# Last feed-forward group multiplied with the tokens on the partitions: an attention and feed-forward block in one kernel

## The chip, the cores and the metric

The kernel runs on one core of a Trainium2 chip. The metric is the device time of one execution in microseconds (us). The core has a matrix engine, TensorE (PE in the profile; its weight loads are listed as PEld), a vector engine, VectorE (DVE), a scalar engine, ScalarE (ACT), GpSimd (POOL), and SyncE (SP), whose queue issues all DMA transfers here. Each engine works through its own instructions in order and waits on semaphores for the others. SBUF is the on-chip memory with 128 partitions, PSUM the accumulator memory that TensorE writes, in eight banks of 512 float32 per partition.

## The reference

The input is 16 sequences of 256 tokens with 256 features, all float32. One block is computed:

```
x = x + layernorm(attention(layernorm(x)))    # 16 heads of 128, causal, biases on q, k, v and the output
x = x + layernorm(ffn(layernorm(x)))          # 256 -> 2048 -> 256, weights stored as 4-bit codes with scales

q, k, v = x @ W_Q[h] + b_Q[h], ...            # per head
attn    = softmax(causal(q k^T / sqrt(128)))
out     = sum over heads of (attn v) @ W_O[h] + b_O

gate, up = x @ Wg^T, x @ Wu^T
out      = (gelu(gate) * up) @ Wd^T
```

Layernorm has no gain and no bias.

## The kernel before

**Splitting.** [...] Each operand is held as a high part (rounded by a copy) and a low part (the operand minus its high part), and `mm3` (L352) issues three matmuls: high by high, high by low, low by high. Products that stay whole float32, such as one 128x128 block of the scores, are issued as one matmul that the profile lists as two instructions.

**Order.** The kernel writes every engine's order out by hand. `run` (L95) issues each instruction behind the last one of every engine, so that the order in the program is the order on each engine; `dma` (L86) does the same for the transfers, all on SyncE's queue. Side work sits in queues of jobs (`urgent`, `behind`, `spare` and others), from which `slot` takes a step at fixed places.

**Attention.** The 4096 tokens are eight blocks of 512 (two sequences). A unit is one head of one block; there are N = 128, numbered by u. The loop at L1021 runs a pipeline over the units: `st_s` makes the scores and the softmax of unit i + 4 (GpSimd scales the probabilities, tile pr), `st_t` and `st_w` turn them in 32x32 pieces and through DRAM, `st_b` loads them as pt, `st_p` (L481) splits pt of unit i + 1 into ph and pl, `st_z` (L490) multiplies unit i with v into pz and splits the result into zh and zl, and `st_o` adds a head's output product. In `st_p`, ScalarE copies 128x512 numbers to ph and GpSimd subtracts to pl. In the last units the feed-forward part begins between them: `x_ops` splits its input, and the first products run (tiles pa, pd, pf).

**Feed-forward.** Four super-blocks of 1024 tokens (two blocks, bb = 0 and 1) by eight groups of 256 hidden features give 32 groups k (loop L1079). The products of gate and up for the four quarters (two halves c of the hidden features by two blocks) are formed by seven products m1 to m7 instead of eight. `Two.done` sends each quarter through a chain: VectorE adds, ScalarE applies gelu, VectorE multiplies by up, ScalarE copies the high part (CAST inter), VectorE subtracts to the low part. The steps wait in the queue `pending`; `part` issues one or two of them with each product, and `quarter` (L868) issues what a later product needs. `st_d(k, bb, dh)` (L877) multiplies group k's quarters by the down weights, six matmuls of 512 tokens, and adds them to a PSUM bank that holds output features (half dh) on the partitions and tokens along the free axis: banks po0 and po1 for block 0, pv and pz for block 1.

**The end.** In the last super-block group 31 isn't multiplied by `st_d` but in `st_last` (L918). It first issues what is left in `pending`: at that point the cast and the low part of quarter (c = 0, bb = 1), then the gelu, the product, the cast and the low part of quarter (c = 1, bb = 0). Then it takes four half blocks n (block 1's two, then block 0's two) of 256 tokens. `multiply` adds the last group's products for one dh into the bank, six matmuls of 256 tokens, and ScalarE copies the 128x256 result to SBUF (oT). `turn_and_measure` turns four 128x128 pieces back with TensorE (transposes into tpo), and VectorE takes the layernorm statistics (bn_stats, bn_aggr, adding epsilon), GpSimd the power -0.5. `apply` computes nb on VectorE, scales and adds the residual x1 on VectorE (xs), adds the shift on ScalarE and issues the output: one transfer of 256 KB for each of the first three halves, two of 128 KB for the last. Statistics of half n - 1 lie between the two products of half n, and half n - 2 is applied behind them.

Of the kernel before, what the change touches and what calls it, by code (L numbers as in the profile page):

```python
# [10 lines left out]
F32 = mybir.dt.float32  # L11
# [3 lines left out]
AF = mybir.ActivationFunctionType  # L15
# [3 lines left out]
P = 128  # L19
# [9 lines left out]
def kernel(  # L29
# [30 lines left out]
    def f(ap):  # L60
        return ap.bitcast(F32)
# [24 lines left out]
    def dma(dst, src):  # L86
        if queue[0] is None:
            queue[0] = nc.sync.dma_start(dst, src).ins
            return
        with tc.issue_after(queue[0]):  # L90
            queue[0] = nc.sync.dma_start(dst, src).ins
# [3 lines left out]
    def run(op, dst, *args, **kw):  # L95
        with ExitStack() as behind:
            for m in last.values():
                behind.enter_context(tc.issue_after(m))
            ins = op(dst, *args, **kw)  # L99
        last[ins.ins.engine] = ins.ins  # L100
        return ins
# [23 lines left out]
    def add(jobs, job, kind):  # L125
        jobs.append([job, 0, kind])
# [24 lines left out]
    def half(t, b, hf):  # L151
        r = b * TB + hf * S
        return t[r : r + S, :].rearrange("(t p) d -> p t d", p=P)

    def ln_stats(srcs):

        n = len(srcs)
        st = small.tile([P, 4, 6], F32, tag="st", name="st")
        mv = small.tile([P, 4, 2], F32, tag="mv", name="mv")
        rs = small.tile([P, 4], F32, tag="rs", name="rs")  # L160
        for t in range(n):
            run(nc.vector.bn_stats, st[:, t, :], srcs[t])
            if t % 2:
                yield V_
        for t in range(n):
            run(nc.vector.bn_aggr, mv[:, t, :], st[:, t, :])
        run(nc.vector.tensor_scalar, rs[:, :n], mv[:, :n, 1], EPS, None, ALU.add)
        yield G_
        run(nc.gpsimd.tensor_tensor, rs[:, :n], rs[:, :n], mhalf[:, :n], ALU.pow)
        return mv, rs  # L170
# [23 lines left out]
    def wide(name):  # L194
        return work.tile([P, 4, D], F32, tag="wide", name=name, bufs=4)
# [156 lines left out]
    def mm3(o, terms, passes=STATIONARY_LAST, start=True, stop=True, shared=False, lows_last=False):  # L352

        todo = [(lhs(a), rhs(c)) for lhs, rhs in terms for a, c in passes]
        if lows_last:
            todo = [todo[m] for m in (0, 1, 3, 4, 2, 5)]
        for i, (lhs, rhs) in enumerate(todo):
            run(
                nc.tensor.matmul, o, lhs, rhs, start=start and i == 0, stop=stop and i == len(todo) - 1, skip_group_check=shared
            )  # L360
# [120 lines left out]
    def st_p(u):  # L481
        pt = PT.pop(u).rearrange("p a m i -> p m a i")
        ph = work.tile([P, 2, 2, P], F32R, tag="ph", name="ph")
        pl = work.tile([P, 2, 2, P], F32R, tag="pl", name="pl")
        four = [t.rearrange("p c b (a i) -> p (c b) a i", a=4) for t in (ph, pl)]
        run(nc.scalar.copy, four[0], pt[:, 0:4])
        run(nc.gpsimd.tensor_tensor, four[1], pt[:, 0:4], f(four[0]), ALU.subtract)
        PH[u] = (ph, pl, pt)

    def st_z(u):  # L490
# [386 lines left out]
    def st_d(k, bb, dh):  # L877


        if not 0 <= k < NGRP:  # L880
            return
        sb, g = divmod(k, NG)
        b = 2 * sb + bb
        w = FW[k, "d"]
        tags = (("po0", "po1"), ("pv", "pz"))[bb]
        if g == 0:
            ACC[b, dh] = ps.tile([P, TB], F32, tag=tags[dh], name="pd")
        po = ACC[b, dh]
        cols = slice(dh * P, (dh + 1) * P)
        i = [quarter(k, c, bb) for c in range(2)]  # L890
        mm3(
            po, [(lambda a, c=c: w[:, a, c, cols], lambda s, c=c: i[c][:, s]) for c in range(2)], MOVING_LAST,
            start=g == 0, stop=g == NG - 1, shared=True,
        )
        if g == NG - 1:
            if dh == 0:
                ACC[b] = back_tile()
            back(ACC[b], dh, po)
            if dh == 1:
                add((urgent, behind)[bb], end(b, ACC.pop(b)), N_)  # L900

    def end(b, tr):
# [12 lines left out]
        for hf in range(2):  # L915
            dma(half(out, b, hf), X1[b][hf])

    def st_last():  # L918


        k = NGRP - 1
        while pending:
            run(*pending.popleft())
        w = FW[k, "d"]
        halves = [(bb, hf) for bb in (1, 0) for hf in range(2)]
        oTs, os, stats = {}, {}, {}

        def multiply(n, dh):
            bb, hf = halves[n]
            tok = slice(hf * S, (hf + 1) * S)  # L930
            cols = slice(dh * P, (dh + 1) * P)
            i = [quarter(k, c, bb) for c in range(2)]
            po = ACC[2 * NSB - 2 + bb, dh][:, tok]
            mm3(
                po, [(lambda a, c=c: w[:, a, c, cols], lambda s, c=c: i[c][:, s, tok]) for c in range(2)], MOVING_LAST,
                start=False, shared=True,
            )
            if dh == 0:
                oTs[n] = wide("oT").rearrange("p a b -> p (a b)")[:, 0 : 2 * S].rearrange("p (h n) -> p h n", h=2)
            run(nc.scalar.copy, oTs[n][:, dh], po)  # L940

        def turn_and_measure(n):
            tp = ps.tile([P, 2, D], F32, tag=("pk", "pq", "sc", "sc")[n], name="tpo", bufs=2 if n > 1 else 1)
            oT = oTs.pop(n)
            for t in range(2):
                for dh in range(2):
                    run(
                        nc.tensor.transpose,
                        tp[:, t, dh * P : (dh + 1) * P], oT[:, dh, t * P : (t + 1) * P], ident,
                    )  # L950
            os[n] = [tp[:, t, :] for t in range(2)]
            jobs = deque()
            stats[n] = None

            def measure():
                stats[n] = yield from ln_stats(os[n])

            add(jobs, measure(), V_)
            finish(jobs)

        def apply(n):
            bb, hf = halves[n]
            b = 2 * NSB - 2 + bb
            mv, rs = stats.pop(n)
            nb = ln_shift(mv, rs, 2)
            x1 = X1[b][hf]
            for t in range(2):
                run(
                    nc.vector.scalar_tensor_tensor,
                    x1[:, t, :], os[n][t], rs[:, t : t + 1], x1[:, t, :], ALU.mult, ALU.add,  # L970
                )
                run(nc.scalar.activation, x1[:, t, :], x1[:, t, :], AF.Identity, bias=nb[:, t : t + 1])
                if n == len(halves) - 1:
                    dma(half(out, b, hf)[:, t, :], x1[:, t, :])
            if n < len(halves) - 1:
                dma(half(out, b, hf), x1)

        count = len(halves)
        for n in range(count + 2):
            if n < count:  # L980
                multiply(n, 0)
            if 0 <= n - 1 < count:
                turn_and_measure(n - 1)
            if n < count:
                multiply(n, 1)
            if n >= 2:
                apply(n - 2)


    first = first_tokens()  # L990
# [84 lines left out]
    def parts(k, *names):  # L1075
        for name in names:
            part(k, name)

    for k in range(NGRP):  # L1079
        sb, g = divmod(k, NG)  # L1080
        if g == 2 and sb + 1 < NSB:
            while not {(0, 2 * sb + 2), (0, 2 * sb + 3)} <= ready:
                step(behind)
            add(spare, x_ops(sb + 1), N_)
        if g == NG - 1:
            for b in (2 * sb, 2 * sb + 1):
                X1[b] = [x_load(x1d, b, hf, ("pr", "tr")[b % 2]) for hf in range(2)]
        if k > 0:
            parts(k, "m1", "m2")
        st_d(k - 1, 1, 0)  # L1090
        for at, n in (k, "d"), (k + 1, "g"), (k + 1, "u"):
            f_get(at, n)
        slot(V_)
        slot(A_ + G_)
        if k > 0:
            parts(k, "m6")
            parts(k, "m5")
        slot(V_)
        slot(A_ + G_)
        st_d(k - 1, 1, 1)  # L1100
        slot(V_)
        slot(A_ + G_)
        if k > 0:
            parts(k, "m7", "m3")
        if k == NGRP - 1:
            parts(k, "m4")
        st_d(k - 1, 0, 0)
        slot(V_)
        slot(A_ + G_)
        if k < NGRP - 1:  # L1110
            parts(k, "m4")
        st_d(k - 1, 0, 1)
        slot(V_)
        slot(A_ + G_)
    finish(urgent)
    finish(behind)
    st_last()


# [49 lines left out]
```

## Time and profile before

| | us |
|---|---|
| median of 3 runs (1517.84 to 1518.86) | 1517.89 |
| the profiled execution | 1517.91 |
| its span, first to last instruction | 1516.1 |
| TensorE busy | 1498.9 |
| VectorE, ScalarE, GpSimd busy | 1185.8, 1037.0, 728.9 |
| last matmuls (transposes of half 3) begin | 1508.61 |
| last output transfer issued | 1513.2 |

The mean granted clock of TensorE is 0.998. Rows of the profile give a start, a duration, the engine, the line, the operation, "out<-in" by tile names, the shape and a count, and in brackets the engine's idle time before it with what ended it. Because all instructions go through the helper `run`, their line is L99 throughout, and a step is known by its tiles: pl is the low part of the probabilities, inter a quarter's high or low part, pd the output banks, oT the copied sums, tpo the turned ones, st, mv, rs and nb the statistics, xs or x1 the residual. Matmuls overlap in the rows; the distance of their starts is what one costs.

### The profile page before, as it was taken

The page shows a single profiled execution, that of the slowest core. Times are in us where ns is not written, and L with a number is a line of the kernel's source. Part 1 is how long each engine was busy: PE and PEld are TensorE (multiplying, and loading weights), DVE is VectorE, ACT ScalarE, POOL GpSimd, SP SyncE. Part 2 cuts the span into 40 slices and gives each one's busy share as a digit, 9 for nine tenths or more (in the row PEclk, how much of TensorE's full clock was granted, in tenths as well). Part 3 has the DMA queues.
Part 4 walks back from the last instruction along what each step waited for, and adds up shares of the span by engine and source line. Part 5 has one row for each costly group of instructions (what it writes and reads, how often), then busy time and mean ns, then how long its engine had stood idle before and what let it go on. Part 6 is the DMA issues. An engine that isn't in the chain of part 4 may idle for free.

```text
span 1516.1 us, 25754 instructions
## 1 busy us (share of the span) xinstructions
PE 1498.9 (99%) x7831; PEld 1278.7 (84%) x7831; DVE 1185.8 (78%) x3011; ACT 1037.0 (68%) x2614; POOL 728.9 (48%) x951
## 2 busy tenths in 40 slices
PE   8999999999999999999999999999999999999997
PEld 7888888888888888888888888887888888888886
DVE  6876787787787888788778787777887887787866
ACT  6877766777677677676677767676766665666565
POOL 3755578677667776866876876880000000000000
PEclk9999999999999999999999999999999999999999
DMA  8998899999899999899899999977557465655561
GB/s 292 339 319 264 262 305 312 286 306 312 281 294 326 282 315 310 274 318 305 274 285 314 306 296 320 316 239 272 210 193 262 182 248 196 250 180 198 219 233 58
DMA packets 200426, 407.55 MB, mean 269 GB/s; under 512 B 21472, under 2 KB 128480, under 8 KB 189536
## 3 DMA queue, kind: packets, MB, share of 16 engines
q1 hardware_dynamic: 200288, 405.91, 79.9%
q8 instruction: 62, 1.02, 0.3%
q14 instruction: 76, 0.62, 0.1%
HBM read 294.15 MB, written 111.67 MB: 268 GB/s over the span
## 4 chain that ended last, share of the span: by engine, by line
PE 94%; DVE 2%; ACT 1%; DMA 1%; POOL 1%; issue 1%; SPq 0%; POOLq 0%; DVEq 0%; ACTq 0%
PE pd L99 13%; PE pk L99 11%; PE pv L99 11%; PE pq L99 11%; PE po L99 11%; PE pz L99 10%; PE sc L99 9%; PE pa L99 8%; PE pf L99 5%; PE pe L99 2%; DVE sum L99 1%; DMA rawq<-in_wq 0%; DMA rawv<-in_wv 0%; ACT pr L99 0%; DVE inter L99 0%
## 5 line engine op out<-in xcount | busy, mean ns | idle before, releaser
L99 POOL TENSOR_SCALAR pr<-pr,rc 128x128 f32<-128x128 f32 (+1 forms) x512 | 250.1, 504 | 90.7 <-DVE rc L99 90.7
L99 ACT ACTIVATE pr<-sc,mn 128x128 f32<-128x128 f32 (+1 forms) x512 | 208.2, 419 | 87.5 <-DVE mn L99 87.5
L99 POOL TENSOR_TENSOR rs<-rs,mhalf 128x4 f32<-128x4 f32 (+1 forms) x35 | 34.5, 985 | 485.1 <-DVE rs L99 275.0
L99 POOL TENSOR_TENSOR pl<-pt,ph 128x512 fp32r<-128x512 f32 x128 | 165.0, 1289 | 190.0 <-ACT ph L99 178.0
L99 DVE CUSTOM_DVE_ANT_0 sc<-sc,mask 128x128 f32<-128x128 f32 (+1 forms) x512 | 180.8, 374 | 67.8 <-PE sc L99 59.1
L99 PE MATMUL pv<-wv,xT 128*128 128x512 f32 x768 | 208.9, 407 | 0.0
L99 ACT ACTIVATE zh<-pz,bqk 128x512 fp32r<-128x512 f32 x128 | 88.3, 690 | 167.7 <-PE pz L99 167.6
L99 PE MATMUL pk<-xT,wk 128*128 128x512 f32 x768 | 199.5, 395 | 0.3 <-POOL xT L99 0.2
L99 PE MATMUL pd<-inter,wd 128*128 128x512 f32 (+1 forms) x792 | 197.8, 385 | 1.4 <-ACT inter L99 1.0
L99 PE MATMUL pq<-xT,wq 128*128 128x512 f32 x768 | 196.3, 391 | 0.0
L99 PEld LDWEIGHTS pd<-inter,wd 128*128 128x128 f32 x792 | 144.9, 188 | 34.5 <-DVE inter L99 2.9
L99 PEld LDWEIGHTS pq<-xT,wq 128*128 128x128 f32 x768 | 144.2, 188 | 32.9
L99 ACT COPY part<-pa 128x512 f32<-128x512 f32 x192 | 111.6, 585 | 68.0 <-PE pa L99 65.5
L99 PE MATMUL po<-zh,wo 128*128 128x512 f32 x512 | 157.7, 389 | 0.0
L99 PEld LDWEIGHTS pk<-xT,wk 128*128 128x128 f32 x768 | 134.9, 188 | 23.8 <-POOL xT L99 0.7
L99 PEld LDWEIGHTS pv<-wv,xT 128*128 128x128 f32 x768 | 135.0, 189 | 23.6
L99 DVE SCALAR_TENSOR_TENSOR zl<-pz,bqk,zh 128x512 fp32r<-128x512 f32 x128 | 95.9, 749 | 74.0 <-ACT zh L99 73.9
L99 ACT CAST inter<-sum 128x512 fp32r<-128x512 f32 x128 | 80.1, 626 | 87.5 <-DVE sum L99 87.5
L99 DVE TENSOR_TENSOR inter<-sum,inter 128x512 fp32r<-128x512 f32 x128 | 89.0, 695 | 56.9 <-ACT inter L99 55.9
L99 DVE STREAM_TRANSPOSE tr<-pr 128x768 f32<-128x768 f32 x128 | 123.3, 963 | 1.7 <-DMA hop<-tr 1.2
L99 DVE SCALAR_TENSOR_TENSOR kl<-pk,bqk,kh 128x512 fp32r<-128x512 f32 x128 | 96.1, 751 | 30.7 <-ACT kr L99 26.9
L99 PEld LDWEIGHTS po<-zh,wo 128*128 128x128 f32 x512 | 96.0, 188 | 19.9
(149 smaller groups left out, 3723.0 us busy)
## 6 DMA issues: line engine op xcount, KB each, us to landing
hop<-tr SPq DMA_DIRECT2D x512, 96.0 KB
pt<-hop SPq DMA_DIRECT2D x128, 384.0 KB
wk<-wk SPq DMA_DIRECT2D x64, 512.0 KB
wq<-wq SPq DMA_DIRECT2D x64, 512.0 KB
wo<-wo SPq DMA_DIRECT2D x64, 512.0 KB
wu<-fu SPq DMA_DIRECT2D x32, 1024.0 KB
wg<-fg SPq DMA_DIRECT2D x32, 1024.0 KB
wv<-wv SPq DMA_DIRECT2D x56, 512.0 KB
```

Of the source, the lines that this page charges most:

```text
L99: ins = op(dst, *args, **kw)
```

## The change

There are two edits.

1. In `st_p`, the low part pl of the last four units (u >= 124) is computed by VectorE instead of GpSimd.
2. The last group's products are formed with the tokens on the partitions. The sums of groups 0 to 30 are copied whole to SBUF by ScalarE (`copy_last(bb)`, two copies of 128x512) and turned by `base_last(bb)`: eight float32 matmuls against the identity for each block, which write four 128x128 pieces into each of two banks (`BASE`), 128 tokens by 256 features twice. `multiply` then adds group 31's products to these banks with the hidden values as the stationary operand and the down weights (256 wide) as the moving one: twelve matmuls for each half block. The statistics read the banks. The copies of each half's result and its transposes are gone. `copy_last(1)` stands behind block 1's last `st_d`, `base_last(1)` behind m4, `copy_last(0)` ahead of `st_last`, and `base_last(0)` behind the products of half 1.

`apply` changes too. For halves 0 to 2 ScalarE computes the scaled and shifted value from PSUM into a new tile fa, and the residual is added by GpSimd (the first piece of every half and the second of half 2) or by VectorE (the second pieces of halves 0 and 1, kept in `rest` and issued behind everything of half 2). Half 3 is applied as before. Every piece of 128 tokens has its own output transfer of 128 KB, eight in all. Statistics of half n now follow the products of half n at once, and half n - 1 is applied behind them.

```diff
-        run(nc.gpsimd.tensor_tensor, four[1], pt[:, 0:4], f(four[0]), ALU.subtract)
+        engine = nc.vector if u >= N - 4 else nc.gpsimd
+        run(engine.tensor_tensor, four[1], pt[:, 0:4], f(four[0]), ALU.subtract)
...
+    LAST = [2 * NSB - 2, 2 * NSB - 1]
+    def copy_last(bb):
+        OT[bb] = wide("oT").rearrange("p a b -> p (a b)").rearrange("p (h n) -> p h n", h=2)
+        for dh in range(2):
+            run(nc.scalar.copy, OT[bb][:, dh], ACC.pop((LAST[bb], dh)))
+    def base_last(bb):
+        oT = OT.pop(bb)
+        for hf in range(2):
+            to = BASE[bb, hf] = ps.tile([P, 2, D], F32, tag=(("po0", "po1"), ("pv", "pz"))[bb][hf], name="base")
+            for t in range(2):
+                for dh in range(2):
+                    run(
+                        nc.tensor.matmul, to[:, t, dh * P : (dh + 1) * P],
+                        oT[:, dh, (2 * hf + t) * P : (2 * hf + t + 1) * P], ident,
+                        start=t == 0 and dh == 0, stop=False, skip_group_check=True,
+                    )
...
-        def multiply(n, dh):
+        def multiply(n):
...
+            for t in range(2):
+                tok = slice((2 * hf + t) * P, (2 * hf + t + 1) * P)
+                mm3(
+                    BASE[bb, hf][:, t, :],
+                    [(lambda s, c=c: i[c][:, s, tok], lambda a, c=c: w[:, a, c, :]) for c in range(2)],
+                    start=False, shared=True,
+                )
...
+        def measure(n):
+            jobs = deque()
+            o = [BASE[halves[n]][:, t, :] for t in range(2)]
+            def work_():
+                mv, rs = yield from ln_stats(o)
+                stats[n] = o, mv, rs
+            add(jobs, work_(), V_)
+            finish(jobs)
         def apply(n):
...
+            if n < 3:
+                fa = wide("fa")
+                for t in range(2):
+                    ln_apply_act(fa[:, t, :], o[t], nb, rs, t)
+                    where = nc.vector if t and n < 2 else nc.gpsimd
+                    todo = (where.tensor_tensor, x1[:, t, :], x1[:, t, :], fa[:, t, :], ALU.add)
+                    if where is nc.vector:
+                        rest.append((todo, to[:, t, :], x1[:, t, :]))
+                    else:
+                        run(*todo)
+                        dma(to[:, t, :], x1[:, t, :])
...
+        for n in range(4):
+            multiply(n)
+            if n == 1:
+                base_last(0)
+            measure(n)
+            if n:
+                apply(n - 1)
+        for todo, to, x1 in rest:
+            run(*todo)
+            dma(to, x1)
+        apply(3)
...
         st_d(k - 1, 1, 1)
+        if k == NGRP - 1:
+            copy_last(1)
...
             parts(k, "m4")
+            base_last(1)
         st_d(k - 1, 0, 0)
...
     finish(behind)
+    copy_last(0)
     st_last()
```

More of the change, by code (lines that the diff above doesn't have):

```diff
@@ L916, in end @@
             dma(half(out, b, hf), X1[b][hf])
+    OT = {}
+    BASE = {}
+    LAST = [2 * NSB - 2, 2 * NSB - 1]
[14 more added lines that the diff above has]
+                    )
     def st_last():
@@ L925, in st_last @@
         halves = [(bb, hf) for bb in (1, 0) for hf in range(2)]
-        oTs, os, stats = {}, {}, {}
-        def multiply(n, dh):
+        stats, sums = {}, {}
+        rest = []
+        def multiply(n):
             bb, hf = halves[n]
-            tok = slice(hf * S, (hf + 1) * S)
-            cols = slice(dh * P, (dh + 1) * P)
             i = [quarter(k, c, bb) for c in range(2)]
[L933 to L944, printed above, removed]
-            for t in range(2):
[L946 to L951, printed above, removed]
-            jobs = deque()
[L953 to L958, printed above, removed]
+            for t in range(2):
+                tok = slice((2 * hf + t) * P, (2 * hf + t + 1) * P)
[5 more added lines that the diff above has]
+        def measure(n):
+            jobs = deque()
+            o = [BASE[halves[n]][:, t, :] for t in range(2)]
[3 more added lines that the diff above has]
+            add(jobs, work_(), V_)
             finish(jobs)
@@ L962, in apply @@
             bb, hf = halves[n]
-            b = 2 * NSB - 2 + bb
-            mv, rs = stats.pop(n)
+            o, mv, rs = stats.pop(n)
             nb = ln_shift(mv, rs, 2)
[L966 to L987, printed above, removed]
+            x1 = X1[LAST[bb]][hf]
+            to = half(out, LAST[bb], hf)
+            if n < 3:
[9 more added lines that the diff above has]
+                        dma(to[:, t, :], x1[:, t, :])
+            else:
+                for t in range(2):
+                    run(
+                        nc.vector.scalar_tensor_tensor,
+                        x1[:, t, :], o[t], rs[:, t : t + 1], x1[:, t, :], ALU.mult, ALU.add,
+                    )
+                    run(nc.scalar.activation, x1[:, t, :], x1[:, t, :], AF.Identity, bias=nb[:, t : t + 1])
+                    dma(to[:, t, :], x1[:, t, :])
+        for n in range(4):
[9 more added lines that the diff above has]
+        apply(3)
     first = first_tokens()
```

## The prediction

> **What bounds the kernel now.** I read the page first, then who TensorE waited for, then the timeline at the two places that the change touches. On the page TensorE is busy in 99% of the span, and the chain that ended last is 94% TensorE.
>
> ```profile
> span 1516.1 us, 25754 instructions
> PE 1498.9 (99%) x7831; PEld 1278.7 (84%) x7831; DVE 1185.8 (78%) x3011; ACT 1037.0 (68%) x2614; POOL 728.9 (48%) x951
> ```
>
> So work that leaves the other engines gains only where TensorE waits for it or after its last matmul; matmuls that are added cost their full time unless they fall into a wait. The answer on TensorE's waits has one that names the low part of the probabilities:
>
> ```profile
> PE pz L99 <- POOL pl L99: 0.9, 1, 0.9
> ```
>
> The timeline places it, in TensorE's and then in GpSimd's rows:
>
> ```profile
> 1009.20 0.28 PE L99 MATMUL pz<-ph,vl 128*128 128x256 f32 x1
> 1010.36 0.39 PE L99 MATMUL pz<-pl,vh 128*128 128x256 f32 x1 [0.88 <-POOL pl L99]
> ...
> 1018.18 0.28 PE L99 MATMUL pz<-ph,vl 128*128 128x256 f32 x1
> 1018.48 0.39 PE L99 MATMUL pz<-pl,vh 128*128 128x256 f32 x1
> ```
>
> ```profile
> 1006.62 2.45 POOL L99 TENSOR_SCALAR xn<-xs,mv,rs 128x256 f32<-128x256 f32 x2
> 1009.04 1.26 POOL L99 TENSOR_TENSOR pl<-pt,ph 128x512 fp32r<-128x512 f32 x1
> ```
>
> Undisturbed, pz<-pl follows pz<-ph,vl by 0.115 us, so 1.04 us are lost for unit 124 and 0.19 for unit 126: GpSimd began pl late, behind two xn. At the end of the kernel I read TensorE and ScalarE side by side:
>
> ```profile
> 1496.87 0.39 PE L99 MATMUL pe<-xl,wu 128*128 128x512 f32 x1
> 1497.10 3.53 PE L99 MATMUL pd<-inter,wd 128*128 128x512 f32 x14
> 1500.86 2.51 PE L99 MATMUL pd<-inter,wd 128*128 128x256 f32 x16 [0.22 <-DVE inter L99]
> ```
>
> ```profile
> 1496.88 0.62 ACT L99 CAST inter<-sum 128x512 fp32r<-128x512 f32 x1 [1.91 <-DVE sum L99]
> 1497.41 0.62 ACT L99 ACTIVATE sum<-sum 128x512 f32<-128x512 f32 x1
> 1499.46 0.62 ACT L99 CAST inter<-sum 128x512 fp32r<-128x512 f32 x1 [1.43 <-DVE sum L99]
> 1499.99 0.63 ACT L99 ACTIVATE sum<-sum 128x512 f32<-128x512 f32 x1
> 1501.44 0.62 ACT L99 CAST inter<-sum 128x512 fp32r<-128x512 f32 x1 [0.82 <-DVE sum L99]
> ```
>
> From 1494.4 the chain leaves TensorE and runs through VectorE and ScalarE. Twelve matmuls of group 30 (1497.10 to 1499.98) run beside it, and at 1500.13 TensorE waits for the cast of 1499.46. I call that cast's start t = 0. The end, in the chain and SyncE's rows:
>
> ```profile
> 1511.64 0.16 DVE nb L99
> 1511.80 0.41 DVEq L1165
> 1512.21 0.02 issue
> 1512.23 0.51 ACT xs L99
> ```
>
> ```profile
> 1512.19 0.37 SPq L91 DMA_DIRECT2D out<-xs  x1
> 1512.76 0.84 SPq L91 DMA_DIRECT2D out<-xs  x2
> ```
>
> Before, the last statistics begin at t = 10.14 (1509.60), the last output DMA is issued at 1513.22 (t = 13.76) and the span ends at t = 16.64. Two issues with nothing to wait for stand 0.46 us apart (four hop<-tr fill 1.84). The outputs' bytes pass at about 340 GB/s until 1514.65, and 1.45 us follow.
>
> **Part 1, pl of units 124 to 127 by VectorE.** Four GpSimd operations (1.29 us) go; four VectorE ones of 128x512 with both inputs in SBUF come, 0.69 each (inter<-sum,inter). Each stands right behind zl of the unit before: for unit 124 at 1008.2, done at 1008.9, and TensorE wants it at 1009.3, so all of the 1.04 can go. Queued behind it on VectorE are the transposes of xn, which wait for GpSimd until 1009.07 anyway. GpSimd's splits of x move up by one pl each, and VectorE idles 0.7 to 1.9 us before each zl there. What is late next: the same rows hold VectorE operations with two SBUF inputs at 1.72 and 1.73 us (1012.97, 1017.24, 1021.09), each beside a GpSimd operation with two inputs, while v<-codes,t at 1004.00 took 0.67 beside pr. With pl gone from GpSimd, its wk, wd and wq stand there, and the wait passes from "sum behind pl" to "sum behind wd". Followed through: unit 125's zh, behind the gelu on ScalarE, comes only about 0.3 us earlier than now, and pl of 126 then costs TensorE some 0.4 again; sum behind wd would end near 1019.4 instead of 1018.97, the cast behind it holds zh of 126, and pl of 127 costs up to another 0.5. Ends: a gain of 1.2 (both stalls gone) and a loss of 0.5 (held as in the 1.73 rows twice over). I take a gain of 0.7: the large stall goes, half of what follows returns. The rows after 1033 are bound by TensorE, so what is gained is kept.
>
> The Trainium skill speaks against this part: GPSIMD Engine Reference, section Specifications, says that GpSimd's interface to SBUF is shared with VectorE, with contention where a VectorE operation has two SBUF inputs. By it alone pl on VectorE would meet xn too and end at 1009.7 instead of 1008.9, a gain of 0.6 at unit 124; the row at 1004.00 does not bear that out for one-input GpSimd work.
>
> **Part 2, the turned sums.** copy_last(1): two ScalarE copies of 128x512 (0.59, one each 0.47) between 1492.0 and 1492.9, ahead of the copy that now starts at 1493.00; that one waits for TensorE until then, so they cost nothing (0.6 if the first were late). base_last(1): eight products of 128x128 float32 against the identity, ahead of group 30's last twelve. The nearest row is sc<-kr,qr, also float32 128x128 and two instructions each: five instructions of one score block recur every 0.57 us (499.95, 500.52), three of them 256 wide at 0.115, which leaves 0.23 a product. Eight make X = 1.84. Bounds: 0.115 a product, the pitch of today's transposes (X = 0.92), and 0.38, the row's own span of a pair (X = 3.04); I take 0.23 since it is the same operation among others. Nothing hides them: TensorE has run dry of other work there.
>
> **Part 3, the hold on ScalarE.** copy_last(0) stands in program order before the pending casts are flushed, so its second copy waits for the last matmul of group 30, and the cast c0b1, the gelu and the last cast wait behind it. The twelve start at 1497.10 + 1.84 = 1498.94, take 2.72 and end with their tail at 1501.82; copy at 1501.86, cast 0.47 later: t = 0 moves from 1499.46 to 1502.33, +2.87. This is the largest term: 1.03 is the copy and its wait, 1.84 the turns.
>
> **Part 4, from t on.** What goes: eight ScalarE copies of 0.37, sixteen transposes, and their handovers; the matmul count stays at 48 of 256 columns. Now, in t: low part c0b1 ready 1.34; products of half 0 end 2.5, half 1 3.9; base_last(0), 1.84 more, 5.75; half 2 at 7.3 (with tail), half 3 at 8.7. VectorE is free of the last low part at 3.3: statistics at 3.3, 4.4, 7.35, 8.75 (1.15 each by today's rows). The third now waits for TensorE, and nb of half 1, queued behind it, for 2.8 us too. The gain over 10.14 is 1.4. It is lost behind: GpSimd gets four adds of 128x256 (0.73, between 0.46 at 128x128 and 1.29 at 128x512) in its queue with the powers. Power 3 waits for rs at 9.9 and add 1 and runs 10.1 to 10.8; half 2's adds run to 11.53 and 12.25. SyncE issues in program order: the second piece of half 2 at 12.3, and behind it the two pieces left for VectorE and the two of half 3, though half 3 itself is ready at 11.9 to 12.1: 12.3 + 4 x 0.46 gives the last issue at 14.1. From there 0.65 to the first byte, 0.385 for 128 KB, 1.45: the end at t = 16.6 (before 16.64). At the ends for the add the last issue moves by -0.5 or +1.1, which the range holds. Eight issues replace five; only the last four, queued, are paid. Two VectorE adds of 0.42 stand before nb of half 3 and are hidden by power 3; if GpSimd holds them, 0.8.
>
> **Sum.** Tail 2.87 - 0.02 = +2.85; part 1 -0.7; span 1516.1 + 2.15 = 1518.25. Around the span lie 1517.91 - 1516.1 = 1.81, and the profiled 1517.91 is the median's 1517.89 within 0.02: **1520.0 us**. With X in the formula the change is 2X - 0.83 - 0.7: X stands before t and again before half 2.
>
> **Rivals.**
> 1. Slower by over 0.2% (3.0 us, about what a measurement of this kernel can tell from no change): the turns cost more than 0.286 us each. At 0.38 it is 2 x 3.04 - 1.53 = +4.55, 1522.4. For it: nothing in the trace shows float32 products eight in a row, with no 256-wide ones between to cover their weight loads. Against: the loads' pitch is 0.11 in every row. Chance 0.15.
> 2. Part 1 turns to its loss of 0.5: +3.35, 1521.2, slower too; this decides once the loss passes 0.2. For it: the three rows of 1.7. Against: VectorE's idle time. Chance 0.20.
> 3. The hold does not happen, because the copies run after the flush or the casts do not stand behind them: -0.02 - 0.7, 1517.2, no change. Against: the listing's order is the engines' order in all rows I followed. 0.07.
> 4. Faster by over 0.2%: it would need no hold, no queue of issues (-2.1) and all of part 1, and comes to 1514.6. 0.05.
> My forecast, 0.53, has its own range of 1518.9 to 1520.9.
>
> **Numbers.** Faster 0.05; same 0.53 + 0.07 and 0.01 of rival 2's mild end; slower the rest, 0.34. Range 1518.2 to 1522.4: rivals 1 and 2 up to their values, the forecast whole; rivals 3 and 4 and the tails are left out.
>
> **What will show it.** Right: ScalarE idle before two pd copies until about 1501, the cast after them; pairs of 128x128 products 0.23 apart; the third statistics waiting for TensorE; five output issues in a row at the end. Wrong: casts at their old distance from the pe products, pz still waiting at unit 124, or turns at another pitch.

## The result, and the profile after

The changed kernel takes 1522.1 us (median of 13 runs, 1520.87 to 1524.6). The kernel before, run beside it, took 1519.03 (13 runs, 1517.84 to 1520.66). The ratio is 1.002, with an interval from 1.0013 to 1.0027: slower by 3.07 us, with an interval that lies clear of 1 and around the 0.2% (3.0 us) that the prediction took as the bound between same and slower. The profiled execution took 1522.26, its span 1520.4.

To see where the time went I cut each span at three rows that every version has: the first product pz of unit 124, the first product pa<-wk,wg behind the last pz, and the last product pe<-xl,wu (1009.09, 1023.34 and 1496.87 before; 1009.77, 1023.45 and 1497.59 after). Part A lies between the first two and holds what edit 1 can move; part C, from the last pe to the end, holds what edit 2 can move (its turns of block 1 follow that product; only the two copies ahead of them come earlier, and ScalarE's next copy still starts 3.87 ahead of the last pe, as before).

| us | to unit 124's first pz | A | between | C | span |
|---|---|---|---|---|---|
| before | 1009.09 | 14.25 | 473.53 | 19.23 | 1516.1 |
| after | 1009.77 | 13.68 | 474.14 | 22.81 | 1520.4 |
| difference | +0.68 | -0.57 | +0.61 | +3.58 | +4.3 |

A and C repeat: five later profiles of kernels with the old end have C at 19.17 to 19.28. The two other stretches hold code that is the same, and differ by up to 2 us from profile to profile; the stretch between A and C comes up again under the late weights. A and C together give +3.01, which the medians' +3.07 bears out.

The page after shows TensorE as the bound still, with 16 more matmuls and 2.9 us more of it:

```profile
span 1520.4 us, 25793 instructions
PE 1501.8 (99%) x7847; PEld 1281.1 (84%) x7847; DVE 1188.3 (78%) x3011; ACT 1038.1 (68%) x2610; POOL 727.4 (48%) x951
```

Attention's end, in the timeline of TensorE: pz<-pl of unit 124 now follows its neighbour by 0.12 us, where it followed by 1.16.

```profile
1009.89 0.28 PE L99 MATMUL pz<-ph,vl 128*128 128x256 f32 x1
1010.01 0.28 PE L99 MATMUL pz<-pl,vh 128*128 128x256 f32 x1
```

The same place in the timeline of VectorE, and then GpSimd's row beside the last of these:

```profile
1008.90 0.75 DVE L99 TENSOR_TENSOR pl<-pt,ph 128x512 fp32r<-128x512 f32 x1
...
1017.44 0.68 DVE L99 TENSOR_TENSOR pl<-pt,ph 128x512 fp32r<-128x512 f32 x1
1018.04 1.78 DVE L99 TENSOR_TENSOR sum<-sum 128x512 f32<-128x512 f32 x1
```

```profile
1017.85 1.43 POOL L99 TENSOR_TENSOR wd<-full,wd 128x512 fp32r<-128x512 f32 x1 [1.69 <-ACT wd L99]
```

The sum takes 1.78 us (1.73 before), now beside wd instead of pl, and the 0.6 of pl stands ahead of it. At the kernel's end, TensorE and then ScalarE in the timeline:

```profile
1497.59 0.40 PE L99 MATMUL pe<-xl,wu 128*128 128x512 f32 x1
1497.82 1.95 PE L99 MATMUL base<-ident,oT 128*128 128x128 f32 x16
1499.52 3.01 PE L99 MATMUL pd<-inter,wd 128*128 128x512 f32 x12
1503.73 0.50 PE L99 MATMUL base<-wd,inter 128*128 128x256 f32 x2 [1.19 <-ACT inter L99]
1504.45 2.90 PE L99 MATMUL base<-wd,inter 128*128 128x256 f32 x22 [0.22 <-DVE inter L99]
1507.19 1.95 PE L99 MATMUL base<-ident,oT 128*128 128x128 f32 x16
1508.90 3.12 PE L99 MATMUL base<-wd,inter 128*128 128x256 f32 x24
```

```profile
1501.19 0.59 ACT L99 COPY oT<-pd 128x512 f32<-128x512 f32 x1 [2.44 <-PE pd L99]
1502.57 0.59 ACT L99 COPY oT<-pd 128x512 f32<-128x512 f32 x1 [0.79 <-PE pd L99]
1503.05 0.62 ACT L99 CAST inter<-sum 128x512 fp32r<-128x512 f32 x1
```

ScalarE stands idle for two copies, and the cast behind them starts 5.46 us after the last pe began, where it started 2.59 after. TensorE waits 1.19 for that cast; before, the two products behind the cast began at 1500.13, and their row lists no wait. Further on, the third statistics wait for TensorE, in VectorE's timeline:

```profile
1510.62 0.76 DVE L99 BATCH_NORM_STATS2 st<-base 128x6 f32<-128x256 f32 x2 [1.98 <-PE base L99]
```

Behind the last product, the timeline of GpSimd and of SyncE's queue:

```profile
1513.51 0.82 POOL L99 TENSOR_TENSOR rs<-rs,mhalf 128x2 f32<-128x2 f32 x1 [0.17 <-DVE nb L99]
1514.31 1.40 POOL L99 TENSOR_TENSOR xs<-xs,fa 128x256 f32<-128x256 f32 x2
```

```profile
1515.74 1.30 SPq L91 DMA_DIRECT2D out<-xs  x3
...
1517.63 0.40 SPq L91 DMA_DIRECT2D out<-xs  x1
```

GpSimd's second add ends at 1515.71. The transfer that waits for it is issued at 1515.74, and four more behind it, the last at 1517.63, though ScalarE had finished the last piece at 1516.39.

### The profile page after: what moved, and what is told of

It is laid out like the page before. It is cut to its first block, busy times and chain, and to the rows that moved or that the text cites. A ratio compares the mean times of both kernels' runs of the same rounds, so it can differ in the third digit from the quotient of the medians.

```text
span 1520.4 us, 25793 instructions
## 1 busy us (share of the span) xinstructions
PE 1501.8 (99%) x7847; PEld 1281.1 (84%) x7847; DVE 1188.3 (78%) x3011; ACT 1038.1 (68%) x2610; POOL 727.4 (48%) x951
## 4 chain that ended last, share of the span: by engine, by line
PE 91%; DMA 2%; DVE 2%; ACT 2%; POOL 1%; issue 0%; SPq 0%; DVEq 0%; ACTq 0%; POOLq 0%
PE pd L99 13%; PE pk L99 11%; PE pv L99 11%; PE pq L99 11%; PE po L99 11%; PE pz L99 9%; PE sc L99 9%; PE pa L99 8%; PE pf L99 5%; PE pe L99 2%; DMA wu<-fu 1%; DVE sum L99 1%; PE base L99 1%; SPq L91 0%; ACT pr L99 0%
## 5 line engine op out<-in xcount | busy, mean ns | idle before, releaser
L99 POOL TENSOR_TENSOR pl<-pt,ph 128x512 fp32r<-128x512 f32 x124 | 160.1, 1291 | 185.1 <-ACT ph L99 174.6
L99 PE MATMUL pd<-inter,wd 128*128 128x512 f32 x744 | 190.7, 391 | 1.0 <-ACT inter L99 1.0
L99 PEld LDWEIGHTS pd<-inter,wd 128*128 128x128 f32 x744 | 138.8, 188 | 33.2 <-DVE inter L99 2.4
```

## The experiments

All ratios are to the kernel before, run on the same chip in the same batch; "rows" are the parts A and C of the profile, less those of before (14.25 and 19.23).

| what runs | median, us | less before's | rows A | rows C | A + C |
|---|---|---|---|---|---|
| the change | 1522.1 | +3.07 | -0.57 | +3.58 | +3.01 |
| edit 1 alone | 1518.32 | -0.73 | -0.57 | -0.03 | -0.60 |
| edit 2 alone | 1522.24 | +3.19 | +0.01 | +3.77 | +3.78 |
| copies behind the casts | 1520.28 | +1.23 | -0.58 | +1.62 | +1.04 |
| turns as transposes | 1519.77 | +0.72 | -0.58 | +1.79 | +1.21 |
| both of these | 1518.7 | -0.12 | -0.59 | -0.11 | -0.70 |
| outputs on two queues | 1521.28 | +2.46 | -0.59 | +2.60 | +2.01 |
| edit 1 for unit 124 alone | 1517.54 | -1.28 | -1.13 | -0.02 | -1.15 |
| the same once more | 1517.98 | -1.15 | -1.15 | -0.06 | -1.21 |
| edit 1, loads issued earlier | 1519.06 | +0.24 | -0.58 | -0.04 | -0.62 |
| unit 124, both mended, outputs as ready | 1518.1 | -1.03 | -1.12 | -0.34 | -1.46 |
| the end written anew | 1516.47 | -2.82 | -1.14 | -1.53 | -2.67 |

One median is sure to about 1.4 us, so where a verdict turns on less I go by the rows, which repeat within 0.1.

### Each edit alone

The first kernel is the kernel before with edit 1; the second is the changed kernel without it:

```diff
-        engine = nc.vector if u >= N - 4 else nc.gpsimd
+        engine = nc.gpsimd
```

> The kernel before with the first edit alone: pl of units 124 to 127 by VectorE. If the prediction's part 1 holds, unit 124's pz no longer waits (1.04 us), some 0.4 is given back at units 126 and 127, and the whole is 0.6 us faster (1517.3 against 1517.9 where the kernel before takes 1517.9), all of it between the first po of unit 124 and the last pz. The rival (VectorE and GpSimd shut each other out, a loss of 0.5) expects +0.5, with VectorE rows of 1.7 us for pl itself.

> The changed kernel with pl of all units on GpSimd again, so the new end alone. The theory that the end holds all of the loss expects +3.6 us against the kernel before: +2.87 up to the cast c0b1 and +0.7 behind it; pz of unit 124 waits 0.88 again. A rival that puts part of the loss elsewhere (a wait of a feed-forward product for its weights, 0.65 in the profile of the changed kernel) expects less than +3 and that wait again.

Edit 1 alone: 1518.32, ratio 0.9991 (0.9982 to 1.0). Edit 2 alone: 1522.24, ratio 1.0023 (1.0012 to 1.0033). The two add up to +2.46, the change has +3.07, within what the intervals allow. So the loss is edit 2's, and edit 1 gains 0.57 in part A. The answer on TensorE's waits for edit 2 alone has the old stall back:

```profile
PE pz L99 <- POOL pl L99: 0.9, 1, 0.9
```

In the profile of edit 1 alone TensorE also waits once in the feed-forward part, at the third group's first product with wu, for weights that arrive late; the row comes up again below:

```profile
1047.54 0.93 PE L99 MATMUL pa<-xT,wu 128*128 128x512 f32 x3 [1.38 <-DMA wu<-fu]
```

### The hold on ScalarE: copies behind the casts

```diff
         while pending:
             run(*pending.popleft())
+        copy_last(0)
         w = FW[k, "d"]
...
     finish(behind)
-    copy_last(0)
     st_last()
```

> The changed kernel with block 0's two copies issued behind the pending casts instead of ahead of them. The hold theory expects the cast c0b1 back at 2.4 us behind the last pe product (now 5.2) and TensorE as the next limit: its turns and products then run without a wait from the first turn on, the third statistics begin about 1.9 us earlier, and the time falls by 1.9 us against the changed kernel. The rival that GpSimd's adds and SyncE's queue set the end expects 0 to -0.5; the rival that the hold is the whole loss expects -2.9.

1520.28, ratio 1.0005 (0.9996 to 1.0014); part C falls by 1.96, as expected. Its timeline, TensorE and then ScalarE:

```profile
1497.65 0.40 PE L99 MATMUL pe<-xl,wu 128*128 128x512 f32 x1
...
1499.58 2.98 PE L99 MATMUL pd<-inter,wd 128*128 128x512 f32 x12
1502.40 3.04 PE L99 MATMUL base<-wd,inter 128*128 128x256 f32 x24
```

```profile
1500.22 0.62 ACT L99 CAST inter<-sum 128x512 fp32r<-128x512 f32 x1 [1.43 <-DVE sum L99]
...
1502.73 1.07 ACT L99 COPY oT<-pd 128x512 f32<-128x512 f32 x2
```

The cast is back at 2.57 us behind the last pe, TensorE's 24 products follow without a wait, and the copies run beside them. The hold moved the cast by 2.87, but taking it away returns 1.96: TensorE, which has the 1.70 of turns and the twelve products to do, becomes what is late next.

### The price of the turns: the same turns as transposes

```diff
-                        start=t == 0 and dh == 0, stop=False, skip_group_check=True,
+                        start=t == 0 and dh == 0, stop=False, skip_group_check=True, is_transpose=True,
```

> The changed kernel with the sixteen turns issued as transposes, one pass each, instead of float32 products of two instructions. By the formula 2X - 0.83 the turns count twice: X falls from 1.7 (the changed kernel's profile) to 0.9, so -1.6 us against the changed kernel, half of it at the cast c0b1 and half at the third statistics. If the second block's turns are hidden behind VectorE, -0.8; if the turns hide altogether, 0.

1519.77, ratio 1.0004 (0.9995 to 1.0013); part C falls by 1.79. In its timeline a block's turns are eight instructions that hold TensorE for 0.79 us, instead of sixteen for 1.70:

```profile
1497.82 1.04 PE L99 MATMUL base<-ident,oT 128*128 128x128 f32 x8
1498.61 2.98 PE L99 MATMUL pd<-inter,wd 128*128 128x512 f32 x12
1502.78 0.50 PE L99 MATMUL base<-wd,inter 128*128 128x256 f32 x2 [1.19 <-ACT inter L99]
```

The 1.19 of waiting for the cast stays, since the hold stays. The saving is 2 x 0.91 = 1.82: the turns count twice, as the prediction's formula has it.

### Both mended: where the gain went

```diff
+        copy_last(0)
         w = FW[k, "d"]
...
-    copy_last(0)
     st_last()
...
-                        start=t == 0 and dh == 0, stop=False, skip_group_check=True,
+                        start=t == 0 and dh == 0, stop=False, skip_group_check=True, is_transpose=True,
```

> The changed kernel with both: block 0's copies behind the pending casts, and the turns as transposes. If TensorE's work alone sets the end once the hold is gone (turns 0.8 for each block, twelve matmuls of 512 at 2.8 in all, 48 of 256 at 0.124), the last statistics begin 3.7 us earlier against the last pe product than in the changed kernel: 1518.4 where that one takes 1522.1. If the hold and the turns overlap (one hides behind the other), only 2.3 to 2.6 are gained.

1518.7, ratio 1.0 (0.9991 to 1.0009). Part C falls by 3.69, as expected, to 19.12: the two causes explain all of the loss, and they add. They leave no gain either, though the last statistics now start 10.70 us behind the last pe, in place of 12.73 before (1509.60 - 1496.87). These rows of VectorE's timeline show where the 2.03 went:

```profile
1507.28 0.76 DVE L99 BATCH_NORM_STATS2 st<-base 128x6 f32<-128x256 f32 x2 [0.19 <-PE base L99]
...
1509.59 0.68 DVE L99 SCALAR_TENSOR_TENSOR nb<-mv,rs 128x2 f32<-128x2 f32 x1 [0.26 <-POOL rs L99]
```

GpSimd's two adds for half 2 run from 1509.53 to 1510.93 and hold up even nb, 128x2 numbers, for 0.68 instead of 0.15. Behind the second add five transfers are issued in a row, the last at 1512.85: 5.57 after the last statistics began, where the kernel before needed 3.62 (1513.22 - 1509.60).

### The outputs: half 3 on ScalarE's queue

The changed kernel, with the two pieces of half 3 issued by ScalarE, and SyncE's transfers in the order in which they become ready; half 2's adds by VectorE come behind half 3:

```diff
-                    where = nc.vector if t and n < 2 else nc.gpsimd
+                    where = nc.vector if t or n == 2 else nc.gpsimd
...
-                    dma(to[:, t, :], x1[:, t, :])
+                    run(nc.scalar.dma_start, to[:, t, :], x1[:, t, :])
...
+            if n == 2:
+                add_rest(1)
             measure(n)
             if n:
                 apply(n - 1)
-        for todo, to, x1 in rest:
-            run(*todo)
-            dma(to, x1)
+            if n == 3:
+                add_rest(1)
         apply(3)
+        add_rest(2)
```

(`add_rest(count)` issues the next adds kept in `rest`, each with its transfer.)

> The changed kernel with the outputs reordered: half 3's two transfers go out from ScalarE's queue behind their activations, GpSimd adds only the first pieces of halves 0 and 1, the second piece of half 0 is added and sent before the third statistics, and half 2's two adds follow half 3's on VectorE. If SyncE's row of issues behind GpSimd's adds set the end, the last issue comes 2.2 us earlier against the last statistics and the time falls by 2.2 us against the changed kernel. The rival that half 3's own chain sets the end expects 0 to -0.5.

1521.28, ratio 1.0017 (1.0008 to 1.0026); part C falls by 0.98, which neither expectation had. Its timeline of ScalarE says why:

```profile
1514.02 0.51 ACT L99 ACTIVATE xs<-xs,nb 128x256 f32<-128x256 f32 x1 [0.39 <-DVE xs L99]
1514.56 0.38 ACTq L99 DMA_DIRECT2D out<-xs  x1
1514.99 0.51 ACT L99 ACTIVATE xs<-xs,nb 128x256 f32<-128x256 f32 x1 [0.46 <-DVE xs L99]
1515.53 0.34 ACTq L99 DMA_DIRECT2D out<-xs  x1
```

The issue of the first piece stands between the two activations, which the changed kernel ran back to back (0.91 for both, from 1515.48). SyncE's row of issues is gone as the bound, but half 3's second activation ends no sooner than in the changed kernel (18.83 behind the last pe, 18.80 there), so that the last issue moves from 20.04 to 18.86 behind it. So the row cost about 1 us over the next limit, not the 2.2 that I had put on it.

### Edit 1, unit by unit

```diff
-        engine = nc.vector if u >= N - 4 else nc.gpsimd
+        engine = nc.vector if u == N - 4 else nc.gpsimd
```

The rest is the kernel before.

> The kernel before with pl of unit 124 alone on VectorE. If what the first edit gives back comes from the three later units (each pl on VectorE in front of an operation that then waits for GpSimd), the 1.04 us of unit 124 stay until the last pz and the kernel is 0.9 us faster than before. If it comes from TensorE being early, with other operations not ready, the last pz is reached 0.6 early as with all four. A wait for the weights wu of a feed-forward group, seen in every profile so far in which pl was on VectorE, may take it all back: then 0.

> The kernel of the seventh experiment once more (pl of unit 124 alone on VectorE), since five rounds left its gain open. The part's own rows should again show 13.1 us from unit 124's first pz to the first product behind the last pz (14.25 before, 13.7 with all four units); the time 1.1 us below the kernel before if nothing takes it back, 0 to 0.5 below if a wait for wu does.

1517.54 (0.9996, 0.9988 to 1.0005) and 1517.98 (0.9993, 0.9984 to 1.0002). Neither interval lies clear of 1, but part A is 13.12 and 13.10 in the two profiles, against 13.66 to 13.68 with four units on VectorE and 14.25 without: unit 124 gains 1.13, and the other three give back 0.56. In the timeline of VectorE for unit 124 alone, the row that follows zl of unit 125:

```profile
1011.73 1.72 DVE L99 SCALAR_TENSOR_TENSOR v<-sg,v 128x512 bf16<-128x512 bf16 x1
```

It starts 2.75 us behind unit 124's first pz (1008.98). In the changed kernel pl stands ahead of it, it starts at 3.35 (1013.12) and takes 1.77 all the same, beside GpSimd's wk where it was beside pl. So pl's 0.60 in VectorE's queue comes on top of a collision that stays.

### Are the late weights edit 1's doing?

Edit 1 alone, with the loads of the next group's weights moved to the top of the group's loop:

```diff
+        for at, n in (k, "d"), (k + 1, "g"), (k + 1, "u"):
+            f_get(at, n)
         if k > 0:
             parts(k, "m1", "m2")
         st_d(k - 1, 1, 0)
-        for at, n in (k, "d"), (k + 1, "g"), (k + 1, "u"):
-            f_get(at, n)
```

> The first edit alone, and the loads of each feed-forward group's weights issued before the group's first two products instead of behind six further matmuls, some 4 us earlier. If the gain of the first edit is taken back by wu landing late (waits of 0.3 to 1.4 us in the four profiles with the edit, none in the two without), those waits are gone and it is 1.3 us faster than the kernel before instead of 0.7. If the waits are chance and cost little in the median, it stays at -0.7.

1519.06, ratio 1.0003 (0.9994 to 1.0012). The expectation was missed: the wait is there still, 1.53 us. The timelines of TensorE and of SyncE's queue:

```profile
1049.01 0.93 PE L99 MATMUL pa<-xT,wu 128*128 128x512 f32 x3 [1.53 <-DMA wu<-fu]
```

```profile
1036.41 0.34 SPq L91 DMA_DIRECT2D o<-ohop  x1
...
1038.77 0.44 SPq L91 DMA_DIRECT2D wu<-fu  x1
```

SyncE issues in order, and the load stood behind o<-ohop, whose issue waits until an earlier transfer has landed; moving it in the program did not move it forward in time (15.3 behind the end of part A, where edit 1 alone has 13.9).

> The kernel before, unchanged, for a second profile. If the wait at the third group's first product with wu belongs to kernels in which TensorE comes earlier to it, there is none here, as in the first profile; if the loads' landing alone decides, it may show a wait of some tenths. The span should lie within 1 us of 1516.1, and the end of the kernel 19.2 us behind the last pe product.

One run of the kernel before, 1519.84, with a span of 1518.1. Its answer on TensorE's waits, and the row in TensorE's timeline:

```profile
PE pa L99 <- DMA wu<-fu: 0.2, 1, 0.2
```

```profile
1411.40 0.94 PE L99 MATMUL pa<-xT,wu 128*128 128x512 f32 x3 [0.23 <-DMA wu<-fu]
```

So the kernel before has such a wait too, if a short one and at a much later product; at the third group's (1048.50) it has none, as in its first profile. The last kernel below, with one unit on VectorE, has one of 0.42 at the same later place. With four units such a wait was seen in all seven profiles, from 0.2 to 1.5 us (in one the releaser shown is a ScalarE row), and in six of them it stands at the third group's product, where none of the seven profiles with one unit or none has any. The stretch between parts A and C agrees with that: 474.06 to 475.62 in the seven profiles with four units (mean 474.8), 473.53 to 474.37 in the seven others (mean 473.8). So in the profiles four units on VectorE went with about 1 us more behind part A, which is more than the 0.57 that they gain in it. Why is not shown: apart from the kernel with the moved loads, these weights were issued 13.6 to 13.9 behind the end of part A in both groups. The medians do not settle it either; those of the kernels with four units lie 0.5 below to 0.9 above what their rows A and C give.

### Putting it together

First try: unit 124 alone, both causes mended, the outputs issued in the order in which they become ready, and half 2 added by VectorE (as in the kernel with two queues, but all on SyncE). Against the kernel with both causes mended:

```diff
-        engine = nc.vector if u >= N - 4 else nc.gpsimd
+        engine = nc.vector if u == N - 4 else nc.gpsimd
...
-                    where = nc.vector if t and n < 2 else nc.gpsimd
+                    where = nc.vector if t or n == 2 else nc.gpsimd
...
+                    if t:
+                        add_rest(1)
                     dma(to[:, t, :], x1[:, t, :])
...
+            if n == 2:
+                add_rest(1)
             measure(n)
             if n:
                 apply(n - 1)
-        for todo, to, x1 in rest:
-            run(*todo)
-            dma(to, x1)
+        add_rest(2)
         apply(3)
```

> What the earlier runs point to, together: pl of unit 124 alone on VectorE; block 0's copies behind the pending casts; turns as transposes; outputs as their pieces come ready (second piece of half 0 added and sent before the third statistics, half 2's first piece added while VectorE waits for the last power, its second behind half 3's products, all on SyncE's queue). The end of the fifth experiment reached the time of the kernel before; the order of outputs gave 1.0 there and should give 1.4 here without transfers issued by ScalarE; unit 124 gives 1.1. Expected 2.5 us below the kernel before, 1516.3 where that takes 1518.8. The rival that waits for wu take what unit 124 gives expects -1.4.

1518.1, ratio 0.9993 (0.9984 to 1.0002): part C fell by 0.34 where 1.4 was expected. The timeline of VectorE:

```profile
1505.06 0.70 DVE L99 TENSOR_TENSOR xs<-xs,fa 128x256 f32<-128x256 f32 x1 [1.09 <-ACT fa L99]
1505.68 0.75 DVE L99 BATCH_NORM_STATS2 st<-base 128x6 f32<-128x256 f32 x2
...
1509.49 0.43 DVE L99 TENSOR_TENSOR xs<-xs,fa 128x256 f32<-128x256 f32 x1 [0.68 <-ACT fa L99]
1509.84 0.15 DVE L99 SCALAR_TENSOR_TENSOR nb<-mv,rs 128x2 f32<-128x2 f32 x1
```

The add for half 0 took 0.70 beside GpSimd's add instead of 0.41, and pushed the third statistics from 9.26 to 9.87 behind the last pe; the add for half 2 stood ahead of nb of half 3. I had moved the work to where another engine held the same thing up.

Second try, with these two rows in mind: half 0's first piece goes to VectorE, before GpSimd has anything to add, and halves 2 and 3 are applied by VectorE from PSUM, half 2 with one transfer of 256 KB. Against the kernel with both causes mended again:

```diff
-        engine = nc.vector if u >= N - 4 else nc.gpsimd
+        engine = nc.vector if u == N - 4 else nc.gpsimd
...
-            if n < 3:
+            if n < 2:
...
-                    where = nc.vector if t and n < 2 else nc.gpsimd
+                    where = nc.vector if t == n else nc.gpsimd
...
-                    if where is nc.vector:
+                    if n and t:
                         rest.append((todo, to[:, t, :], x1[:, t, :]))
...
-                    dma(to[:, t, :], x1[:, t, :])
+                    if n == 3:
+                        dma(to[:, t, :], x1[:, t, :])
+                if n == 2:
+                    dma(to, x1)
...
             measure(n)
+            if n == 3:
+                add_rest(1)
             if n:
                 apply(n - 1)
-        for todo, to, x1 in rest:
-            run(*todo)
-            dma(to, x1)
```

> Unit 124's low part alone on VectorE; copies behind the casts, turns as transposes; and the end written anew so that no output waits in a row behind a late add. Half 0's first piece is added by VectorE while it waits for the third half's products, its second by GpSimd; half 1's first by GpSimd, its second by VectorE behind the last statistics; halves 2 and 3 are scaled and added by VectorE from PSUM as the kernel before does, half 2 in one transfer of 256 KB. Theory (in the end of the run with both faults undone, 2.03 us earlier statistics were spent again on GpSimd's last two adds, on nb beside them at 0.68 instead of 0.15, and on five transfers issued in a row): by that run's rows, the low number of half 3 starts at about 1509.8 there, its two scalings end at 1510.7, ScalarE's shifts at 1510.85 and 1511.25, the last transfer is issued 14.7 us after the last product pe and the span ends 17.5 us after it (before 19.2, both faults undone 19.1); attention's end 13.1 us. Median 2.8 below the kernel before: 0.998. Rival (VectorE is now the bound, as in the run that put adds early): an add beside GpSimd's takes 0.70 and pushes the third statistics, the end comes 18.5 to 18.9 us after the last pe, and the median lies 1.5 to 2 below.

1516.47, ratio 0.9982 (0.9973 to 0.9991): 2.82 us faster than the kernel before and the only version whose interval lies clear of 1 on that side. Part C is 17.70 (expected 17.5), part A 13.11. The timeline of VectorE, then that of SyncE's queue:

```profile
1505.40 0.43 DVE L99 TENSOR_TENSOR xs<-xs,fa 128x256 f32<-128x256 f32 x1 [0.63 <-ACT fa L99]
1505.82 0.76 DVE L99 BATCH_NORM_STATS2 st<-base 128x6 f32<-128x256 f32 x2
...
1509.68 0.14 DVE L99 SCALAR_TENSOR_TENSOR nb<-mv,rs 128x2 f32<-128x2 f32 x1
1509.75 0.86 DVE L99 SCALAR_TENSOR_TENSOR xs<-base,rs,xs 128x256 f32<-128x256 f32 x2
```

```profile
1505.85 5.87 SPq L91 DMA_DIRECT2D out<-xs  x7
```

The first add fits into VectorE's wait for the third statistics (9.22 behind the last pe, 1496.60), nb takes 0.14, and seven issues replace eight, with the last at 14.7 behind the last pe, where the kernel before has 16.35 (1513.22 - 1496.87).

## Why the prediction was right, and which terms were not

The forecast was 1520.0, within 0.2% of before, and the time 1522.1 lies in its range. It does not lie in the forecast's own range (1518.9 to 1520.9), but in the upper part that was there for rivals 1 and 2, and the rows of A and C show neither of them: the order of events was right, and that the whole range held owes something to luck. The predicted difference was +2.1; the measured one is +3.07. So 1.0 of the 2.1 by which the time missed is the change, and 1.1 is the level: the kernel before took 1519.03 in the runs beside the change, not 1517.89.

- **Part 1** was put at a gain of 0.7, between 1.2 and a loss of 0.5. Its rows give 0.57, by the mechanism named: the stall of unit 124 goes whole (1.13 with that unit alone), and half comes back: 0.28 ahead of unit 126's first pz, behind v<-sg,v (1.77, with pl ahead of it), and 0.38 at unit 127, behind the sum that now meets wd (1.78), less 0.15 of the old wait at unit 126. That counts part A alone; the waits for late weights behind it, which the prediction did not have ("what is gained is kept"), may take it back. The rule of the Trainium skill (GPSIMD Engine Reference, Specifications) would have had pl meet xn too. In the row at 1008.90 pl took 0.75 beside xn, and the two xn took 2.45 as before: GpSimd work with one input delayed nothing here, work with two did.
- **Part 2**: turns at 0.23 each, 1.84 a block; they took 1.70, 0.21 each. The copies of block 1 (1492.60 to 1493.71) cost nothing, as said.
- **Part 3**, the hold: +2.87 predicted, 5.46 - 2.59 = 2.87 measured. Two small errors cancel: the turns took 0.14 less, and from the first of the twelve products to the cast 0.14 more passed than reckoned. Copies behind the casts return 1.96 of it.
- **Part 4**, from t on, is the term that was mis-sized: -0.02 predicted, +0.71 measured (the end at t = 17.35 instead of 16.6). Its order of events was right: third statistics at 7.57 (7.35), last at 9.00 (8.75), five issues in a row. Three sizes were short. The 256-wide products with the hidden values as weights stand 0.124 apart instead of 0.115, 0.25 until the last statistics. Power 3 took 0.82 instead of 0.70 and the second add of half 2 ended at t = 12.66 instead of 12.25, so the last issue came at 14.58 instead of 14.1. (Half 3 itself was ready at 12.9 to 13.3 instead of 11.9 to 12.1, with nb at 0.68 beside GpSimd's add; the row of issues hid that.) And from there the end took 2.77 where 2.5 was reckoned from the bytes' 340 GB/s; the last pieces passed at about 260.
- **Sum**: +2.15 predicted for the span; A and C give +3.01, of which 0.73 is part 4 and 0.13 part 1.

**The rivals.** The turns did not reach the 0.286 each from which rival 1 decides (its argument that weight loads stand 0.11 apart "in every row" is not so: beside 512-wide products twelve of them take 2.69 at 1496.88, 0.23 apart); part 1 did not turn to a loss in part A (rival 2); the hold did happen (rival 3), and the kernel with the copies moved shows what is left without it. Rival 4 named what a gain would need: no hold, no row of issues and all of part 1, 3.3 below before. That is the kernel with the end written anew, which came to 2.82 below with the turns made cheaper too. The measured ratio sits on the bound of 0.2% itself, so the chances of "same" and "slower" can't be told apart by it.

## What to carry to other kernels

A copy that waits for TensorE, issued ahead of work queued on the same engine, delays all of that work: look where a new instruction stands in its engine's order before counting what it removes. Earlier statistics or results are worth nothing until the row behind them is followed to the last transfer; here 2 us of it went to two late adds and to issues 0.45 apart, and came back only when these were rebuilt. An operation moved off a busy engine pays at the place where somebody waited for it, one unit of four here, and costs at the others.

## What the hardware showed that I had not expected

- A float32 128x128 turn as a transpose is one instruction, and eight hold TensorE for 0.79 us; as a matmul against the identity it is two, and eight take 1.70.
- VectorE and GpSimd instructions that both read two SBUF tiles held each other up, by their durations about as if one ran behind the other, down to the smallest: nb of 128x2 took 0.68 instead of 0.15 beside an add on GpSimd, an add of 128x256 0.70 instead of 0.41, a sum of 128x512 1.78 instead of 0.68. VectorE's scaling from PSUM with one tile in SBUF was not held up (0.86 for two beside GpSimd's adds).
- Weights of 1 MB landed in time in some profiles and up to 1.4 us late in others, for the same product and with the same order of loads: a wait at that product stands in six of the seven profiles with pl of four units on VectorE (one of them with the loads moved) and in none of the seven others. What makes them late stayed open.
